# A graph network's first layer: the products that reorder a part of the edges issued in one piece, and a place's bits taken by one and-operation

## The chip, the cores and the metric

The kernel runs on one NeuronCore of one Trainium2 chip. The metric is the device time of one execution in microseconds (us), as the median of several executions. A profile of one execution stands beside it; its times are us from its first instruction, unless marked ns. PE is the engine of the matmuls (PEld its weight loads), DVE the vector engine, ACT the scalar engine, POOL the general one (here it issues the gathers of node rows), SP a queue that issues DMA transfers. Each engine works its instructions off in the program's order.

## The reference

A graph of N = 6250 nodes with 64 features and 206250 edges (src, dst), sorted by dst, with 64 attributes each. Three layers of an attention convolution:

```python
q = x @ Wq + bq; k = x @ Wk + bk; v = x @ Wv + bv
e = edge_attr @ We
alpha = sum(q[dst] * (k[src] + e), -1) / sqrt(64)
w = softmax of alpha over the edges of one dst
x = segment_sum((v[src] + e) * w, dst) + x @ Ws + bs
x = relu(x)                      # and a layer norm after layers 0 and 1
...
out = layernorm(x_in + log_softmax(x))
```

## The kernel before

**Tiling.** Edges go in tiles of 128, chunks of 6 tiles (768 edges, which touch at most 32 neighbouring nodes), and units of 4 chunks (LB = 4): 67 whole units and a small rest. In every layer a loop runs over the units. It holds four quarters (j = 0 to 3), one per chunk. In each, PE transposes the chunk's node features (`turn`, L1679, into bank ps_a), and over the quarters the scores of the unit before are made (`scores`, L1692, bank ps_s, in two halves), masked and reduced on DVE (`most`, L1706), exponentiated on ACT (L1720), transposed (`weights`, L1734, bank ps_p), copied to probT by ACT (L1737) and multiplied with the features (`sums`, L1746, bank ps_g). Node rows come in by gathers (POOL) or by **picks**: one-hot matmuls with node features that stay in SBUF (L1387, eight a pick, bank ps_s or ps_p by the quarter), whose result DVE copies out (L1356, L1359, `evacuate`).

**The reordering.** So that later layers can pick rows, layer 0 also puts each unit's edges into an order by their source node. That is the work of a `Move`, one per unit. It has four `Part`s: half h of a chunk's tiles and pair i of chunks (h, i = 0, 0; 0, 1; 1, 0; 1, 1). A part has three **steps** (HT = 3, t = 0 to 2), one tile of each of its two chunks at a time:
- `row` (L1074, DVE) makes two one-hots `hit` of 128 x 384: which place each edge of the tile goes to. They lie in 12 buffers and are made two steps ahead.
- `prepare` (L1042, L1045, DVE) splits the raw edge attributes of the part to come into three bf16 thirds, raw, rest and end.
- `products` (L1077 to L1102, PE) multiplies thirds and one-hots: six matmuls a step into one bank ps_x, two beside each other, one on columns 0 to 63 and one on columns 64 to 127. With the second pair (i = 1) come four more a step into ps_m, one per chunk, 32 columns each: `stamp` holds, for each edge, five bits of its place among the chunk's 32 nodes and numbers of its source. After the third step `drain` (ACT, L1115, L1118) copies ps_m to `to` and ps_x to `eT`, and sends eT to DRAM (L1121).
- `put` does, for the move before: `index` (L1165, L1167) with the first step, `shade` (L1152, from bank ps_m, copied by ACT at L1153) with the second and third step of part 0, and `across` (L1128, transposes of eT into ps_a, copied by ACT at L1136) with two steps each of part 0 and part 1.

**The mark.** For each 16 chunks (four units) `mark` works out the places, in 18 pieces, one a step (L887 to L1014). DVE and PE take turns in it. Its last pieces transpose the edges' places (L999) and break each into five bits: nine operations of 96 elements on DVE (L1008, L1010), written into `misc`, from which ACT fills the stamps (`impress`, L1064, L1065).

**What sets the order.** The order is written out by hand: the generator `sorter` makes one step at each `next`, and the loop of units calls it three times a quarter (`move`, L1817; six times in the first three units), twice ahead of the quarter's pick and once behind it. So one quarter works one part, and one unit one move. Each engine then follows that order and waits for the others only where data or a bank asks for it. Bank tags of PSUM: two buffers each for ps_a and ps_x, one each for ps_m, ps_s, ps_p and ps_g. ps_a serves nearly all transposes, the index and the mark.

Of the kernel before, what the change touches and what calls it, by code (L numbers as in the profile page):

```python
# [10 lines left out]
I32 = mybir.dt.int32  # L11
# [4 lines left out]
ALU = mybir.AluOpType  # L16
# [3 lines left out]
P = 128  # L20
D = 64
# [7 lines left out]
W = 32  # L29
BITS = 5  # L30
FAR = 2.0**100
GS = 4
LB = 4
TC = 6
CE = TC * P
HT = TC // 2
HE = HT * P
# [392 lines left out]
def main_path(  # L430
# [53 lines left out]
    nc = tc.nc  # L484
# [27 lines left out]
    const = ctx.enter_context(tc.tile_pool(name="const", bufs=1))  # L512
# [16 lines left out]
    def ps(tag):  # L529
        return psum.tile([P, 512], F32, tag=tag, name=f"ps_{tag}", bufs={"a": 2, "x": 2}.get(tag, 1))  # L530
# [5 lines left out]
    start = turns.tile([P, NK * CE], F32, name="start")  # L536
# [114 lines left out]
    for k in range(NK):  # L651
        n = min(P, NC - k * P)
# [80 lines left out]
    nc.vector.memset(code, 0.0)  # L733
    for j in range(LB):
        strip = slice(j * W, (j + 1) * W)
        for at in (j * (BITS + 1), P + j * W):
            nc.vector.tensor_copy(code[strip, at : at + BITS + 1], bit[strip, :])
# [108 lines left out]
    kbs = const.tile([P, NT, NP, LB], mybir.dt.uint8, name="kbs")  # L846
    four = const.tile([P, KB], F32, name="four")
    shift = const.tile([P, TC, 2], F32, name="shift")
    stamps = [const.tile([P, LB * TC, W], BF16, name=f"stamp{i}") for i in range(2)]

    def tools():
# [29 lines left out]
        for stamp in stamps:  # L881
            nc.vector.memset(stamp, 0.0)
            nc.vector.memset(stamp[:, :, ROW_ONE], 1.0)

    marks = {}

    def mark(g):  # L887
# [3 lines left out]
        n = m * TC  # L891
# [106 lines left out]
        for t in range(TC):  # L998
# [3 lines left out]
                ident[w0 : w0 + wide, w0 : w0 + wide],  # L1002
            )
        yield
        nc.vector.tensor_copy(v.rearrange("p (c t) -> p c t", t=TC), place)
        for b in reversed(range(BITS)):
            row = misc[:, b]
            nc.vector.tensor_scalar(row, v, 2.0**b, None, ALU.is_ge)  # L1008
            if b:
                nc.vector.scalar_tensor_tensor(v, row, -(2.0**b), v, ALU.mult, ALU.add)  # L1010
            if b == 2:
                yield
        marks[g] = misc, pos
        yield  # L1014

# [32 lines left out]
    class Move:  # L1048
# [25 lines left out]
                nc.vector.tensor_scalar(hit, ruler, self.pos[:, at : at + 1], None, ALU.is_equal)  # L1074
                self.hits[h, c, t] = hit

        def products(self, h, i, t):  # L1077

            if not t:
                self.px = ps("x")  # L1080
                if i:
                    self.pm = ps("m")
            for part in range(3):
                for j in range(2):
                    nc.tensor.matmul(  # L1085
                        self.px[j * D : (j + 1) * D, :HE],
                        self.parts[2 * h + i].thirds[part][:, j, t * D : (t + 1) * D],
                        self.hits[h, 2 * i + j, t],
                        start=(t == 0 and part == 0),
                        stop=(t == HT - 1 and part == 2),  # L1090
                    )
            if i:
                for c in range(LB):
                    nc.tensor.matmul(  # L1094
                        self.pm[c * W : (c + 1) * W, :HE],
                        self.stamp[:, c * TC + h * HT + t, :],
                        self.hits.pop((h, c, t)),
                        start=(t == 0),
                        stop=(t == HT - 1),
                    )  # L1100
            if t == HT - 1:
                self.drain(h, i)  # L1102

        def drain(self, h, i):

# [40 lines left out]
        def shade(self, h):  # L1146

            if not h:
                self.mask = tos.tile([P, CE], BF16, name="mask", bufs=1)
            pm = ps("m")  # L1150
            cols = slice(h * HE, (h + 1) * HE)
            nc.tensor.matmul(pm[:, :HE], codeW, self.to[:, cols], start=True, stop=True)  # L1152
# [51 lines left out]
    def sorter():  # L1204
# [16 lines left out]
        for stage in range(2):  # L1221
            todo[0].prepare(stage)
        moves[0].impress()
        for s in range(2):
            steps[s][0].move.row(steps[s][0].h, steps[s][0].i, steps[s][1])
        opened.append(True)
        yield
# [875 lines left out]
```

## Time and profile before

| | |
|---|---|
| median of 3 runs | 4206.91 us (4202.07 to 4214.05) |
| the profiled execution's own time | 4197.44 us |
| its span, first to last instruction | 4195.7 us |
| PE busy | 3513.2 us, 84% |
| DVE busy | 3452.3 us, 82% |
| ACT busy | 2347.5 us, 56% |
| POOL busy | 2563.3 us, 61% |
| mean granted PE clock | 0.953 |

Layer 0 ends near 1890 us; layers 1 and 2 take the rest. "Busy" counts the time in which an engine has an instruction under way. Idle time in a row's brackets is what the engine waited just before that instruction, with the operation that ended the wait. A row of several equal matmuls (x8) gives their time from the first start to the last end; successive rows of PE overlap, since one matmul drains while the next one runs, so lengths on PE are read from start to start. A float32 matmul counts as two, so a pick or a score product of 4 matmuls in the code is 8 in the trace.

### The profile page before, as it was taken

The page shows a single profiled execution, that of the slowest core. Times are in us where ns is not written, and L with a number is a line of the kernel's source. Part 1 is how long each engine was busy: PE and PEld are TensorE (multiplying, and loading weights), DVE is VectorE, ACT ScalarE, POOL GpSimd, SP SyncE. Part 2 cuts the span into 40 slices and gives each one's busy share as a digit, 9 for nine tenths or more (in the row PEclk, how much of TensorE's full clock was granted, in tenths as well). Part 3 has the DMA queues.
Part 4 walks back from the last instruction along what each step waited for, and adds up shares of the span by engine and source line. Part 5 has one row for each costly group of instructions (what it writes and reads, how often), then busy time and mean ns, then how long its engine had stood idle before and what let it go on. Part 6 is the DMA issues. An engine that isn't in the chain of part 4 may idle for free.

```text
span 4195.7 us, 109920 instructions
## 1 busy us (share of the span) xinstructions
PE 3513.2 (84%) x35239; PEld 2484.7 (59%) x35239; DVE 3452.3 (82%) x12154; ACT 2347.5 (56%) x5994; POOL 2563.3 (61%) x2510
## 2 busy tenths in 40 slices
PE   3878889998998998895988888888858888888886
PEld 2445555555555555553767667666647667666674
DVE  5678898889888898874888888888758888888886
ACT  0445555655565555563655555555535656666665
POOL 5466666666666666663766666666447666666662
PEclk9899999999999999996999999999979999999998
DMA  5666666667666667665777777777648777777774
GB/s 109 177 165 180 174 186 177 175 181 187 179 176 181 178 173 183 180 182 130 189 182 183 182 176 178 192 176 182 164 127 192 185 174 185 187 179 183 179 179 101
DMA packets 779286, 729.02 MB, mean 174 GB/s; under 512 B 483080, under 2 KB 607938, under 8 KB 778704
## 3 DMA queue, kind: packets, MB, share of 16 engines
q1 hardware_dynamic: 630436, 512.79, 49.9%
q0 software_dynamic: 80000, 82.08, 10.2%
q10 hardware_dynamic: 68268, 127.03, 8.4%
q8 instruction: 288, 4.72, 0.5%
q14 instruction: 294, 2.41, 0.2%
HBM read 562.78 MB, written 158.68 MB: 172 GB/s over the span
## 4 chain that ended last, share of the span: by engine, by line


## 5 line engine op out<-in xcount | busy, mean ns | idle before, releaser
L601 POOL DMA_INDIRECT feat<-x,gate x1328 | 1318.0, 992 | 729.0 <-ACT gate L633 356.4
L601 POOL DMA_INDIRECT feat<-in_x,gate x1100 | 1172.1, 1066 | 690.4 <-ACT gate L633 369.6
L1387 PE MATMUL ps_x<-parts,hot 128*128 128x256 f32 x7392 | 1084.9, 294 | 223.1 <-DVE feat L1359 185.9
L1387 PEld LDWEIGHTS ps_x<-parts,hot 128*128 128x128 f32 x7392 | 946.0, 193 | 383.0 <-issue 213.5
L1682 ACT COPY featT<-ps_a 64x384 f32<-64x384 f32 x1588 | 753.8, 475 | 372.9 <-PE ps_a L1679 351.5
L1359 DVE COPY_PREDICATED feat<-which,ps_x 128x128 f32<-128x128 int32 x2772 | 838.0, 302 | 95.5
L1335 DVE TENSOR_SCALAR hot<-keys,rank 128x512 fp32r<-128x512 f16 (+1 forms) x1304 | 507.3, 457 | 4.7 <-DMA keys<-keyS 4.7
L1074 DVE TENSOR_SCALAR hit<-ruler,pos 128x384 bf16<-128x384 f16 x1608 | 456.3, 325 | 6.3 <-PE ps_m L1094 5.4
L1679 PE MATMUL ps_a<-ident,feat 128*128 128x128 f32 x2380 | 420.9, 286 | 40.7 <-DMA feat<-x,src_b 31.9
L1679 PEld LDWEIGHTS ps_a<-ident,feat 128*128 128x128 f32 x2380 | 279.6, 145 | 226.0 <-issue 185.3
L1356 DVE COPY feat<-ps_x 128x128 f32<-128x128 f32 x924 | 263.9, 286 | 173.6 <-PE ps_x L1387 166.4
L1692 PE MATMUL ps_s<-featT,q 128*32 128x384 f32 x2134 | 289.5, 507 | 81.4 <-DMA featT<-eaS 43.1
L1720 ACT ACTIVATE prob<-prob,part 128x768 f32<-128x768 f32 x204 | 190.3, 933 | 232.0 <-DVE part L1719 200.5
L1746 PE MATMUL ps_g<-feat,probT 128*32 128x128 f32 x9672 | 311.7, 275 | 2.4 <-ACT probT L1737 2.4
L1085 PE MATMUL ps_x<-hit,raw 128*64 128x384 bf16 x1608 | 294.5, 362 | 0.5 <-DVE hit L1074 0.4
L1746 PEld LDWEIGHTS ps_g<-feat,probT 128*32 128x32 f32 x9672 | 261.9, 110 | 25.6 <-ACT probT L1737 4.1
L1085 PE MATMUL ps_x<-hit,rest 128*64 128x384 bf16 x1608 | 276.2, 340 | 0.0
L1085 PE MATMUL ps_x<-hit,end 128*64 128x384 bf16 x1608 | 275.6, 339 | 0.0
L1737 ACT COPY probT<-ps_p 128x384 f32<-128x384 f32 x399 | 191.8, 481 | 124.7 <-PE ps_p L1734 92.8
L1734 PE MATMUL ps_p<-ident,prob 128*128 128x128 f32 x1197 | 206.8, 283 | 9.7 <-ACT prob L1720 9.6
L1118 ACT COPY eT<-ps_x 128x384 f32<-128x384 f32 x268 | 129.3, 483 | 122.1 <-PE ps_x L1085 84.7
L1136 ACT COPY feat<-ps_a 128x384 f32<-128x384 f32 x256 | 122.1, 481 | 133.6 <-PE ps_a L1128 97.4
(266 smaller groups left out, 5167.9 us busy)
## 6 DMA issues: line engine op xcount, KB each, us to landing
featT<-eaS SPq DMA_DIRECT2D x792, 192.0 KB
feat<-eaP SPq DMA_DIRECT2D x134, 768.0 KB
keys<-keyS SPq DMA_DIRECT2D x132, 448.0 KB
raw<-in_ea SPq DMA_DIRECT2D x536, 96.0 KB
eaS<-eT ACTq DMA_DIRECT2D x134, 384.0 KB
eaP<-feat ACTq DMA_DIRECT2D x128, 384.0 KB
shade<-maskS SPq DMA_DIRECT2D x198, 192.0 KB
feat<-x,gate POOLq DMA_INDIRECT x1328
```

The lines of the kernel that those rows point to most:

```text
L601: nc.gpsimd.indirect_dma_start(out=feat[:, c, t, 0], out_offset=None, in_=xts[layer][:, :], in_offset=bass.IndirectOffsetOnAxis(ap=index[: ...
L1074: nc.vector.tensor_scalar(hit, ruler, self.pos[:, at : at + 1], None, ALU.is_equal)
L1085: nc.tensor.matmul(self.px[j * D : (j + 1) * D, :HE], self.parts[2 * h + i].thirds[part][:, j, t * D : (t + 1) * D], self.hits[h, 2 * i + ...
L1335: nc.vector.tensor_scalar(hot[:, h], keys[self.layer, k][:, first : first + n], rank[:, h : h + 1], None, ALU.is_equal)
L1356: nc.vector.tensor_copy(found, px[:, :, 0])
L1359: nc.vector.copy_predicated(found, which[:, first : first + 2, b].bitcast(I32).unsqueeze(2).to_broadcast([P, 2, D]), px[:, :, b],)
L1387: nc.tensor.matmul(px[:, v].rearrange("p b d -> p (b d)"), hot[:, h, (2 * pair + v) * P : (2 * pair + v + 1) * P], those[:, i, b0 + h * KB ...
L1679: nc.tensor.transpose(pt[:, t * P : (t + 1) * P], rows[:, 2 * t * D : 2 * (t + 1) * D], ident)
L1682: nc.scalar.copy(featT[:, :, h, :], pt[h * D : (h + 1) * D, : n * P].rearrange("d (i e) -> d i e", e=P))
L1692: nc.tensor.matmul(p_s[rows, :w], self.q[:, rows], self.featT[j][:, cols], start=True, stop=True)
L1734: nc.tensor.transpose(p_t[:, t, :n], self.prob[:n, at : at + P], ident[:n, :n])
L1746: nc.tensor.matmul(p_g[rows, :].rearrange("n (h d) -> n h d", h=2), self.probT[:, t, rows], batch[:, j, t], start=(t == 0), stop=(t == sel ...
```

## The change

Five edits, all in layer 0 or its setting up. `products` is called once a part, at its third step, and issues all of the part: 18 matmuls into ps_x, then 6 into ps_m, those of the part's own two chunks. The bank ps_m is now held from a move's part with i = 0 to the one with i = 1, and `shade` takes ps_a instead. One-hots are made three steps ahead (a part), and the next move's stamps are filled one step sooner. In the mark the five bits come from one and-operation with a table of the powers 1 to 16 and one ACT copy; each bit then stands as 0 or its power, and the table `codeW` that the mask is made with is scaled by the inverse powers (five one-column operations in the setting up, five more fill the powers).

```diff
         nc.vector.tensor_copy(v.rearrange("p (c t) -> p c t", t=TC), place)
-        for b in reversed(range(BITS)):
-            row = misc[:, b]
-            nc.vector.tensor_scalar(row, v, 2.0**b, None, ALU.is_ge)
-            if b:
-                nc.vector.scalar_tensor_tensor(v, row, -(2.0**b), v, ALU.mult, ALU.add)
-            if b == 2:
-                yield
+        bits = spare[:, 1 : BITS + 1].bitcast(I32)
+        nc.vector.tensor_tensor(
+            bits,
+            v.unsqueeze(1).to_broadcast([P, BITS, n]),
+            powers.unsqueeze(2).to_broadcast([P, BITS, n]),
+            ALU.bitwise_and,
+        )
+        nc.scalar.copy(misc[:, :BITS], bits)
+        yield
...
-        def products(self, h, i, t):
-
-            if not t:
-                self.px = ps("x")
-                if i:
-                    self.pm = ps("m")
-            for part in range(3):
-                for j in range(2):
-                    nc.tensor.matmul(
-                        self.px[j * D : (j + 1) * D, :HE],
...
-            if i:
-                for c in range(LB):
+        def products(self, h, i):
+
+            px = self.px = ps("x")
+            if not i:
+                self.pm = ps("m")
+            for t in range(HT):
+                for part in range(3):
+                    for j in range(2):
+                        nc.tensor.matmul(
+                            px[j * D : (j + 1) * D, :HE],
...
+            for t in range(HT):
+                for c in range(2 * i, 2 * i + 2):
                     nc.tensor.matmul(
                         self.pm[c * W : (c + 1) * W, :HE],
                         self.stamp[:, c * TC + h * HT + t, :],
...
-            if t == HT - 1:
-                self.drain(h, i)
+            self.drain(h, i)
...
-            pm = ps("m")
+            pm = ps("a")
...
-                if part is move.parts[3] and not t and n + 1 < len(moves):
+                if part is move.parts[2] and t == HT - 1 and n + 1 < len(moves):
...
-                if s + 2 < len(steps):
-                    ahead_of, u = steps[s + 2]
+                if s + HT < len(steps):
+                    ahead_of, u = steps[s + HT]
...
-                move.products(part.h, part.i, t)
+                if t == HT - 1:
+                    move.products(part.h, part.i)
```

Line numbers below 733 stay. Later lines stand four to ten further on in the changed kernel (`products` 1077 becomes 1087, `turn` 1679 becomes 1689).

**PE, first quarter of a unit, from the chunk's transposes to the next scores.** Before (of rows that repeat, one stands for all; ps_x are the products, L1152 the shade, L1128 the across, L1387 the pick):

```order
L1679 MATMUL ps_a<-ident,feat 128x128 x3
L1165 MATMUL ps_a<-to,keyc 4x4x64
L1167 MATMUL ps_g<-pickc,to 128x12
L1085 MATMUL ps_x<-hit,raw 64x384
L1152 MATMUL ps_m<-to,codeW 128x384
L1128 MATMUL ps_a<-ident,eT 128x128 x3
L1387 MATMUL ps_p<-parts,hot_11341 128x256 x8
L1692 MATMUL ps_s<-featT,q 32x384 x4
```

And with the change:

```order
L1689 MATMUL ps_a<-ident,feat 128x128 x3
L1174 MATMUL ps_a<-to,keyc 4x4x64
L1176 MATMUL ps_g<-pickc,to 128x12
L1161 MATMUL ps_a<-to,codeW 128x384
L1137 MATMUL ps_a<-ident,eT 128x128 x3
L1397 MATMUL ps_p<-parts,hot_11307 128x256 x8
L1095 MATMUL ps_x<-hit,raw 64x384
L1104 MATMUL ps_m<-hit,stamp_265 32x384
L1702 MATMUL ps_s<-featT,q 32x384 x4
```

Before, six products (L1085) stand after the index, six more before the pick, and six after the second pair of shade and across. Now index, shade and across follow each other directly, then the pick, then shade and across once more, and only then all 18 products and the six of the stamps. Every product before the pick in this order now takes ps_a, or ps_g.

**PE, last quarter, from the prob transposes (L1734, with the change L1744) on.** Before:

```order
L1734 MATMUL ps_p<-ident,prob 128x128 x3
L1679 MATMUL ps_a<-ident,feat 128x128 x3
L1085 MATMUL ps_x<-hit,raw 64x384
L1094 MATMUL ps_m<-hit,stamp_259 32x384
L1387 MATMUL ps_p<-parts,hot_24820 128x256 x8
```

And with the change:

```order
L1744 MATMUL ps_p<-ident,prob 128x128 x3
L1689 MATMUL ps_a<-ident,feat 128x128 x3
L1397 MATMUL ps_p<-parts,hot_24737 128x256 x8
L1095 MATMUL ps_x<-hit,raw 64x384
L1104 MATMUL ps_m<-hit,stamp_265 32x384
```

The products of two steps stood between the transposes into ps_p and the pick that uses ps_p again; now only the chunk's three transposes do.

**DVE, the end of the mark.** Before:

```order
L1005 COPY spare<-ps_a 128x96
L1008 TENSOR_SCALAR misc<-spare 128x96
L1010 SCALAR_TENSOR_TENSOR spare<-misc,spare 128x96
L1074 TENSOR_SCALAR hit<-ruler,pos 128x384 x2
L1356 COPY feat<-ps_s 128x2x64
```

And with the change:

```order
L1013 CAST spare<-ps_a 128x96
L1015 TENSOR_TENSOR spare<-spare,powers 128x480
L1084 TENSOR_SCALAR hit<-ruler,pos 128x384 x2
L1366 COPY feat<-ps_s 128x2x64
L1369 COPY_PREDICATED feat<-which,ps_s 128x2x64 x3
```

Nine narrow operations (L1008 five times, L1010 four times, in two groups with the one-hots between) become one of 480 elements. Apart from that DVE's order stays as it was; its one-hots are those of a step further on.

More of the change, by code (lines that the diff above doesn't have):

```diff
@@ L735, in main_path @@
         strip = slice(j * W, (j + 1) * W)
-        for at in (j * (BITS + 1), P + j * W):
-            nc.vector.tensor_copy(code[strip, at : at + BITS + 1], bit[strip, :])
+        nc.vector.tensor_copy(code[strip, j * (BITS + 1) : (j + 1) * (BITS + 1)], bit[strip, :])
+    for b in range(BITS):
+        nc.vector.tensor_scalar(bit[:, b : b + 1], bit[:, b : b + 1], 2.0**-b, None, ALU.mult)
+    for j in range(LB):
+        strip = slice(j * W, (j + 1) * W)
+        nc.vector.tensor_copy(code[strip, P + j * W : P + j * W + BITS + 1], bit[strip, :])
     pc = ps("a")
@@ L883, in tools @@
             nc.vector.memset(stamp[:, :, ROW_ONE], 1.0)
+        for b in range(BITS):
+            nc.vector.memset(powers[:, b : b + 1], 1 << b)
     marks = {}
@@ L1075, in row @@
                 self.hits[h, c, t] = hit
-        def products(self, h, i, t):
-            if not t:
-                self.px = ps("x")
-                if i:
-                    self.pm = ps("m")
-            for part in range(3):
-                for j in range(2):
-                    nc.tensor.matmul(
-                        self.px[j * D : (j + 1) * D, :HE],
[L1087 to L1091, printed above, removed]
-            if i:
-                for c in range(LB):
+        def products(self, h, i):
[7 more added lines that the diff above has]
+                            px[j * D : (j + 1) * D, :HE],
+                            self.parts[2 * h + i].thirds[part][:, j, t * D : (t + 1) * D],
+                            self.hits[h, 2 * i + j, t],
+                            start=(t == 0 and part == 0),
+                            stop=(t == HT - 1 and part == 2),
+                        )
+            for t in range(HT):
+                for c in range(2 * i, 2 * i + 2):
                     nc.tensor.matmul(
@@ L1223, in sorter @@
         moves[0].impress()
-        for s in range(2):
+        for s in range(HT):
             steps[s][0].move.row(steps[s][0].h, steps[s][0].i, steps[s][1])
```

2 lines of the change are left out of this document (added).

## The prediction

> **What bounds the kernel now.** The page's chain of waits is empty, so I read the table of stretches, cut at the start of each unit's sums (L1746), then the waits, then the order of time inside one unit. The change touches layer 0 alone, its loop of units. Four neighbouring units (us from the start, length, then busy time of PE, PEld, DVE, ACT, POOL, the granted clock, DMA):
>
> ```profile
> 1280.29:1302.84 22.55, 21.45 (x237) 13.04 (x233) 17.97 (x63) 14.52 (x38) 15.49 (x16) 1.00 0.88 223
> 1302.84:1333.07 30.23, 25.31 (x259) 14.68 (x251) 28.33 (x96) 15.64 (x41) 23.59 (x20) 1.00 0.64 170
> 1333.07:1362.92 29.85, 24.51 (x244) 14.93 (x245) 25.82 (x92) 15.32 (x42) 13.64 (x15) 0.94 0.55 146
> 1362.92:1385.20 22.28, 21.67 (x240) 13.54 (x236) 19.89 (x70) 14.98 (x39) 16.70 (x17) 1.00 0.81 206
> ```
>
> The pattern repeats: a mark serves 16 chunks, four units, and its 18 steps cover one and a half units of 12. So two units in four are **plain**: PE is busy 21.5 of 22.4 us and sets the length, DVE has over 2 us to spare. In the **first mark unit** DVE (28.3 of 30.2) sets it and PE has 5 us to spare. In the second it goes from DVE to ACT to PE. The waits from 400 to 1700 us (engine, line waited for, us, times, longest) say the same:
>
> ```profile
> PE ps_a L923 <- DVE kinds L916: 23.5, 12, 2.9
> PE ps_s L1692 <- DVE most L1706: 20.6, 25, 1.7
> PE ps_a L1128 <- ACT featT L1682: 14.2, 17, 2.2
> PE ps_a L1165 <- ACT featT L1682: 11.4, 18, 1.0
> DVE feat L1356 <- PE ps_s L1387: 36.1, 54, 1.5
> DVE feat L1356 <- PE ps_p L1387: 19.7, 37, 1.4
> ```
>
> The first two are PE ahead of DVE, in mark units; the next two are PE waiting for ACT to empty one of the two ps_a banks; the last two are DVE waiting for picks, mostly in plain units, where it costs nothing. No row has PE waiting for a one-hot. So what counts is whether PE's work in plain units gets shorter and whether its waits for ACT grow.
>
> **PE's own work.** Five rows of one step (start, length), and two where two steps stand together already:
>
> ```profile
> 1300.03 0.36 PE L1085 MATMUL ps_x<-hit,raw 128*64 128x384 bf16 x2
> 1300.22 0.33 PE L1085 MATMUL ps_x<-hit,rest 128*64 128x384 bf16 x2
> 1300.38 0.33 PE L1085 MATMUL ps_x<-hit,end 128*64 128x384 bf16 x2
> 1300.64 0.35 PE L1094 MATMUL ps_m<-hit,stamp 128*32 128x384 bf16 x4
> 1300.92 1.21 PE L1387 MATMUL ps_p<-parts,hot 128*128 128x256 f32 x8
> ...
> 1355.91 0.33 PE L1085 MATMUL ps_x<-hit,end 128*64 128x384 bf16 x2
> 1356.08 0.33 PE L1085 MATMUL ps_x<-hit,raw 128*64 128x384 bf16 x2
> ```
>
> A pair on the two halves of the columns takes 0.16 us from start to start, and each change to another shape about 0.1 more (0.26, 0.28). A step of i = 0 costs 0.61, one of i = 1 0.89: six of each, 9.0 us a unit. A part in one piece: 0.19 + 7 x 0.163 + 0.26 = 1.59 for nine pairs, so ten shape changes a unit are saved. But the stamps' products stand two beside each other instead of four. Their 24 a unit take 12 rounds instead of 6: three rounds a part, 2 x 0.165 + 0.28 = 0.61. Four parts: 8.8 us, **0.2 us less a unit**. No row shows two strips of 32 returned to at once. If they ran as fast as four abreast it were 0.33 less a part, if one by one at 0.26 then 0.95 more; I take 0.165 because the pairs above return to the same columns after 0.16.
>
> **ps_a in a unit's first quarter.** What the moved steps issue here: index, two shades, two acrosses, with two steps' products between them as filler. PE, then ACT:
>
> ```profile
> 1282.35 0.55 PE L1679 MATMUL ps_a<-ident,feat 128*128 128x128 f32 x3
> ...
> 1283.14 0.31 PE L1167 MATMUL ps_g<-pickc,to 128*128 128x12 bf16 x6
> 1283.37 0.35 PE L1085 MATMUL ps_x<-hit,raw 128*64 128x384 bf16 x2
> ...
> 1283.99 0.34 PE L1152 MATMUL ps_m<-to,codeW 128*128 128x384 bf16 x1
> 1284.16 0.49 PE L1128 MATMUL ps_a<-ident,eT 128*128 128x128 f32 x3
> ...
> 1285.19 1.20 PE L1387 MATMUL ps_p<-parts,hot 128*128 128x256 f32 x8
> 1286.23 0.34 PE L1152 MATMUL ps_m<-to,codeW 128*128 128x384 bf16 x1
> ```
> ```profile
> 1282.93 0.96 ACT L1682 COPY featT<-ps_a 64x384 f32<-64x384 f32 x2 [0.81 <-PE ps_a L1679]
> ...
> 1284.01 0.57 ACT L1186 CAST key<-ps_a 4x512 f16<-4x512 f32 x1
> ...
> 1285.88 0.48 ACT L1136 COPY feat<-ps_a 128x384 f32<-128x384 f32 x1
> ```
>
> Now the shade asks for a ps_a bank, and the filler is gone. PE has the index done at 1283.37; the shade needs the bank of the unit's transposes, free when ACT's featT copies end at 1283.89: 0.52 us of waiting. The shade (0.17) ends at 1284.06; the across needs the keys' bank, copied by 1284.58: 0.52 more. Across (1.03 to the picks, less a step's 0.61) and picks (1.04) run to 1286.04, the second shade to 1286.21, the second across waits for the feat copy's end at 1286.36: 0.15. Together **1.2 us a plain unit**. The products come afterwards with nothing left to hide under. That this bank wait is real the L1165 row above shows: where another transpose stands between, the keys' product waits for these very copies, 18 times, 0.6 us each.
>
> **The last quarter.** The picks there use bank p, just after the prob transposes:
>
> ```profile
> 1298.34 0.55 PE L1734 MATMUL ps_p<-ident,prob 128*128 128x128 f32 x3
> 1298.72 0.49 PE L1679 MATMUL ps_a<-ident,feat 128*128 128x128 f32 x3
> ...
> 1299.14 0.35 PE L1085 MATMUL ps_x<-hit,raw 128*64 128x384 bf16 x2
> ```
> ```profile
> 1298.88 0.48 ACT L1118 COPY eT<-ps_x 128x384 f32<-128x384 f32 x1
> 1299.39 0.33 ACTq L1121 DMA_DIRECT2D eaS<-eT  x1
> 1299.76 0.48 ACT L1737 COPY probT<-ps_p 128x384 f32<-128x384 f32 x1 [0.40 <-issue]
> ```
>
> Two steps' products covered the copy to probT. Now the picks are ready 0.80 us after 1298.34 and must wait for it. ACT still has to do eT (which may start some 0.4 before, when the last pair is done), the issue of eaS and probT: -0.4 + 0.48 + 0.33 + 0.48, about 0.9 to 1.1. I take **0.3 us**; the ends are 0 and 1.1 (with ACT as late as in these rows, done at 1300.24 against 1299.14).
>
> **The mark's bits** (groups from 400 to 1700 us):
>
> ```profile
> L1008 DVE TENSOR_SCALAR misc<-spare 128x96 bf16<-128x96 f32 x65 | 14.4, 221 | 1.8
> L1010 DVE SCALAR_TENSOR_TENSOR spare<-misc,spare 128x96 f32<-128x96 bf16 x52 | 13.7, 264 | 1.8
> L946 DVE TENSOR_TENSOR spare<-ps_a,kinds 128x480 f16<-128x480 f32 x36 | 23.3, 647 | 1.0 <-PE ps_a L944 0.9
> ACT misc L985 <- DVE spare L984: 24.7, 12, 3.4
> ```
>
> Nine operations go, 5 x 221 + 4 x 264 = 2.16 us a mark; one of 480 elements comes. It isn't in the trace; between 0.22 (the narrow row) and 1.1 (five narrow ones) I take L946's 0.65, the same width. DVE saves 1.5 us a mark, 17 marks (268 chunks by 16), 26 us. It falls in the second quarter of the second mark unit, where PE comes out of a wait late and DVE behind it:
>
> ```profile
> 1349.58 0.55 PE L1128 MATMUL ps_a<-ident,eT 128*128 128x128 f32 x3 [2.21 <-ACT featT L1682]
> ...
> 1351.11 2.08 PE L1387 MATMUL ps_s<-parts,hot 128*128 128x256 f32 x8
> 1353.22 0.29 DVE L1356 COPY feat<-ps_s 128x128 f32<-128x128 f32 x1 [1.08 <-PE ps_s L1387]
> ```
>
> DVE waits 1.08 us for the picks just behind the bits, so I count the saving as nothing; without that cover it is the 26 us. The new ACT copy (estimate 0.6 us, by the 384-wide 0.48) must wait for the and-operation with feat, eT and featT copies queued behind it, as misc does at L985 (2 us each time, PE then waits for ps_a). ACT reaches it after the feat copy of the 1349.58 across, DVE sooner: nothing, at worst 15 x 2 = 30 us. In this quarter the step whose products stood in the shadow of the 2.21 us now follows: 0.4 us.
>
> **At nothing.** The one-hots lie in 12 buffers, two parts: each now waits until PE has done nearly the whole part before the last. Behind it on DVE stand rest, end and the copies out of the picks' banks, for which later picks wait. DVE's spare time in plain units covers it; in first mark units PE is ahead. Uncovered it is up to 1 us a quarter there, 60 us. On SP's queue the loads of raw wait for the same part's last reading, four parts before their use, and nothing is late there. Setting up (ten one-column operations, two one-hots sooner): 1 to 3 us.
>
> **Sum.** After the first three units, 61 units: 30 plain, 15 and 15 marked. Plain: -0.2 + 1.2 + 0.3 = 1.3. The L1128 and L1165 waits, 25.6 us over some 49 units, are 0.5 each, and half may fall together with the new ones: 1.05, times 30 = 32 us. First mark unit: 0, since PE's later arrival shortens the waits for L916 and L1706. Second: 0.4 in its second quarter, the last quarter's 0.3, -0.2: 0.5 x 15 = 7. With 1 for setting up, **+40 us**: on the profiled run's 4197.4 that is 4237; on the median of the runs shown, 9.5 above it, 4247.
>
> **Rivals.** (1) **DVE sets more than I think, and it becomes faster.** If the mark units are DVE's to the end, the 26 us come through, and 61 x 0.2 = 12 us of PE's work with them, provided ACT empties ps_a in time: 4207 - 26 - 12 = 4169. Picks ahead of products also shorten the 55.8 us of DVE's waits at L1356. Against it: those waits lie where PE is full, and the ps_a wait has rows. It decides from where the new waits stay under 0.5 us a plain unit. Chance 0.15. (2) **Both cancel**: 30 x 1.05 against 26: within 13 us of 4207. Chance 0.11. (3) **The clock falls more often.** After the 2.21 us wait eight picks took 2.08 us, not 1.21; with its neighbours some 1.4 us. Once more in each of 15 mark units: +21, 4268. PE's idle time is gathered into fewer, longer pieces, which speaks for it; in plain units the new pieces are short and the clock is 1.00. Chance 0.10. By the Trainium skill (TensorE: Matmul & The Clock Gate, Part 1) an idle window of about 3.4 us halves the clock until a busy one has passed; the 2.08 agrees. (4) **Stamps' weights aren't loaded under the products before**: 0.26 a round, not 0.165, 0.2 a part, 0.8 a unit; plain units alone 24 us, 4271. The pairs at 0.16 speak against it. Chance 0.05. The Trainium skill (same page, Part 3, The mechanism) has loads overlap only where the row groups differ, which would be this case; the pairs share their rows and don't wait.
>
> The forecast's own chance is 0.59, its own range 4225 to 4270. Less than 0.3% (13 us) this measurement can't tell from no change. Faster 0.15, same 0.11, slower 0.74. The range, 4185 to 4290, leaves out the best of (1), and the upper ends of the last quarter and the one-hots together.
>
> **What would show it.** Plain units of 23 to 24 us, not 22.4; in them PE waits of about 0.5 us at the shade and the across for ACT's featT and key copies, and at the last picks for probT. The mark's and-operation near 0.65 us, second mark units no shorter, first ones near 30 us. Three stamp rounds in 0.5 to 0.6 us. Plain units at 22 us, or mark units 1.5 us shorter, would prove me wrong; so would DVE waiting long at the one-hots in the first mark unit.

## The result, and the profile after

| | before | after |
|---|---|---|
| median of 4 runs, us | 4210.48 (4202.07 to 4223.55) | 4275.22 (4271.27 to 4280.43) |
| ratio, 95% interval | | 1.0159 (1.0134 to 1.0184) |
| the profiled execution's own time, us | 4197.44 | 4272.08 |
| busy PE / DVE / ACT, us | 3513.2 / 3452.3 / 2347.5 | 3531.2 / 3425.5 / 2357.6 |
| mean granted PE clock | 0.953 | 0.942 |

The change costs 65 us; 40 were forecast. DVE lost 27 us of work, as worked out for the mark's bits, and that bought no time (e1 below). The two profiled executions lie 74 us apart: 57 us up to layer 1's first sums (2001.45 us before, 2058.87 after), and 17 behind them, where nothing was edited. That last stretch took 2194 us before and 2211 after, and 2178 to 2196 in the profiles of e1 to e10, so the 17 us are taken for the scatter of single executions and not for the change.

The table of stretches of the kernel after, cut at the start of each unit's sums (now L1756), has the columns of the prediction's: length, then busy time of PE, PEld, DVE, ACT and POOL, granted clock, DMA share and GB/s. First the four neighbours that answer to the prediction's four, then a plain unit in which a group of nodes is finished beside the usual work:

```profile
1323.08:1345.36 22.28, 20.81 (x236) 14.08 (x237) 17.93 (x63) 14.38 (x38) 16.04 (x16) 1.00 0.88 237
1345.36:1377.88 32.52, 27.30 (x263) 16.80 (x261) 28.34 (x95) 14.96 (x40) 21.72 (x19) 0.95 0.56 147
1377.88:1405.45 27.57, 23.34 (x239) 15.66 (x237) 24.64 (x85) 16.54 (x45) 16.05 (x15) 0.94 0.60 159
1405.45:1428.18 22.73, 21.30 (x240) 14.55 (x240) 19.57 (x70) 14.95 (x39) 16.71 (x16) 1.00 0.80 208
...
662.01:695.11 33.10, 27.15 (x252) 18.74 (x252) 21.56 (x80) 17.54 (x41) 19.27 (x20) 0.80 0.56 150
```

The same finishing unit before:

```profile
647.59:674.54 26.95, 24.96 (x252) 15.69 (x248) 20.40 (x77) 17.40 (x41) 16.68 (x17) 0.94 0.66 175
```

The plain units hardly moved (22.55 and 22.28 before, 22.28 and 22.73 now). The first mark unit is 2.3 us longer, and the finishing unit 6.2 us, at a clock of 0.80. So the bulk isn't where the prediction looked. All 50 units from the 7th on, by kind (numbers counted from 0; means of such lengths, us; "finishing" are the four plain units with products `ve, wT`, L1547):

| | number | before | after | all together |
|---|---|---|---|---|
| plain | 22 | 22.82 | 23.40 | +12.7 |
| finishing | 4 | 25.47 | 30.70 | +20.9 |
| first mark unit | 12 | 30.89 | 32.08 | +14.3 |
| second mark unit | 12 | 28.43 | 28.60 | +2.0 |
| the 50 units | | 1315.8 | 1365.7 | +49.9 |

The first seven units add 11 us (223.9, now 235.0).

PE's waits from 400 to 1700 us (bank, line, what was waited for: us, times, longest) after the change:

```profile
PE ps_p L1397 <- ACT probT L1747: 27.0, 44, 3.2
PE ps_a L1137 <- ACT featT L1692: 22.2, 25, 1.6
PE ps_a L1137 <- ACT key L1195: 17.0, 26, 1.7
PE ps_a L949 <- ACT featT L1692: 15.3, 12, 1.4
...
PE ps_s L1702 <- DVE most L1716: 6.5, 11, 0.7
...
PE ps_a L930 <- DVE kinds L923: 5.4, 5, 2.3
```

The two waits for DVE that led before, 23.5 us for `kinds` and 20.6 for `most`, are down to 5.4 and 6.5. In their place PE waits for ACT to empty a bank, in three places: at the last picks (L1397), at the across (L1137) and at the mark's L949.

### The profile page after: what moved, and what is told of

Its sections match the earlier page's. It is cut to its first block, busy times and chain, and to the rows that moved or that the text cites. A ratio compares the mean times of both kernels' runs of the same rounds, so it can differ in the third digit from the quotient of the medians.

```text
span 4270.0 us, 109764 instructions
## 1 busy us (share of the span) xinstructions
PE 3531.2 (83%) x35239; PEld 2576.5 (60%) x35239; DVE 3425.5 (80%) x12028; ACT 2357.6 (55%) x6011; POOL 2580.1 (60%) x2510
## 4 chain that ended last, share of the span: by engine, by line
## 5 line engine op out<-in xcount | busy, mean ns | idle before, releaser
L601 POOL DMA_INDIRECT feat<-in_x,gate x1100 | 1185.9, 1078 | 734.0 <-ACT gate L633 423.1
L1397 PE MATMUL ps_x<-parts,hot 128*128 128x256 f32 x7392 | 1090.1, 295 | 222.2 <-DVE feat L1369 186.0
L1397 PEld LDWEIGHTS ps_x<-parts,hot 128*128 128x128 f32 x7392 | 952.0, 194 | 382.8 <-issue 214.2
L1084 DVE TENSOR_SCALAR hit<-ruler,pos 128x384 bf16<-128x384 f16 x1608 | 450.7, 321 | 36.0 <-PE ps_m L1104 35.8
L1702 PE MATMUL ps_s<-featT,q 128*32 128x384 f32 x2134 | 321.4, 498 | 67.6 <-DMA featT<-eaS 50.0
L1756 PE MATMUL ps_g<-feat,probT 128*32 128x128 f32 x9672 | 335.2, 276 | 3.6 <-ACT probT L1747 3.6
L1756 PEld LDWEIGHTS ps_g<-feat,probT 128*32 128x32 f32 x9672 | 275.7, 110 | 28.6 <-ACT probT L1747 5.8
L1137 PE MATMUL ps_a<-ident,eT 128*128 128x128 f32 x804 | 156.9, 310 | 86.0 <-ACT featT L1692 25.4
L1124 ACT CAST to<-ps_m 128x384 bf16<-128x384 f32 x134 | 64.2, 479 | 268.6 <-PE ps_m L1104 260.5
L1744 PE MATMUL ps_p<-ident,prob 128*128 128x128 f32 x1197 | 206.1, 282 | 7.7 <-ACT prob L1730 7.6
```

Source lines behind the costliest of these rows:

```text
L601: nc.gpsimd.indirect_dma_start(out=feat[:, c, t, 0], out_offset=None, in_=xts[layer][:, :], in_offset=bass.IndirectOffsetOnAxis(ap=index[: ...
L1397: nc.tensor.matmul(px[:, v].rearrange("p b d -> p (b d)"), hot[:, h, (2 * pair + v) * P : (2 * pair + v + 1) * P], those[:, i, b0 + h * KB ...
L1702: nc.tensor.matmul(p_s[rows, :w], self.q[:, rows], self.featT[j][:, cols], start=True, stop=True)
L1744: nc.tensor.transpose(p_t[:, t, :n], self.prob[:n, at : at + P], ident[:n, :n])
L1756: nc.tensor.matmul(p_g[rows, :].rearrange("n (h d) -> n h d", h=2), self.probT[:, t, rows], batch[:, j, t], start=(t == 0), stop=(t == sel ...
```

## Where the time went in the trace after

A plain unit, PE by time (start, length, line, in brackets the wait):

```profile
1327.21 0.32 PE L1161 MATMUL ps_a<-to,codeW 128*128 128x384 bf16 x1 [0.50 <-ACT featT L1692]
1327.91 0.55 PE L1137 MATMUL ps_a<-ident,eT 128*128 128x128 f32 x3 [0.38 <-ACT key L1195]
...
1336.61 0.67 PE L1104 MATMUL ps_m<-hit,stamp 128*32 128x384 bf16 x6
1337.20 0.55 PE L1744 MATMUL ps_p<-ident,prob 128*128 128x128 f32 x3
...
1342.60 1.22 PE L1397 MATMUL ps_p<-parts,hot 128*128 128x256 f32 x8 [0.58 <-ACT probT L1747]
```

The three waits stand where they were forecast, 0.50, 0.38 and 0.58 us; the one at the second across is missing. Three stamp rounds take 0.59 us, from 1336.61 to 1337.20 (0.61 forecast).

ACT ahead of those last picks, and a row of the kernel before:

```profile
1340.51 0.41 ACT L1074 COPY stamp<-misc 128x120 bf16<-128x120 bf16 x1
1340.83 0.34 ACT L1075 COPY stamp<-misc 128x72 bf16<-128x72 bf16 x1
1341.19 0.48 ACT L1127 COPY eT<-ps_x 128x384 f32<-128x384 f32 x1
...
1342.07 0.48 ACT L1747 COPY probT<-ps_p 128x384 f32<-128x384 f32 x1 [0.40 <-PE ps_a L1689]
```
```profile
1301.22 0.43 ACT L1064 COPY stamp<-misc 128x120 bf16<-128x120 bf16 x1
```

The two copies that fill the next move's stamps come one step sooner with the change. Before, they stood behind probT (1301.22, probT at 1299.76); now they take ACT 0.68 us, from 1340.51 to 1341.19, ahead of eT and so of probT. The prediction's chain for this wait (eT, the issue of eaS, probT) doesn't hold them. Its transposes (L1744) end at 1341.69, so without the copies probT could have started about then and not at 1342.07: an estimate of 0.38 us of the 0.58. No run moved the copies back; e3 and e8 keep them here, under cover of products.

The finishing unit, PE first, then ACT:

```profile
670.87 0.90 PE L1137 MATMUL ps_a<-ident,eT 128*128 128x128 f32 x3 [1.54 <-ACT key L1195]
671.43 2.06 PE L1397 MATMUL ps_p<-parts,hot 128*128 128x256 f32 x8
...
690.07 2.07 PE L1397 MATMUL ps_p<-parts,hot 128*128 128x256 f32 x8 [3.24 <-ACT probT L1747]
692.07 0.53 PE L1095 MATMUL ps_x<-hit,raw 128*64 128x384 bf16 x2
692.39 0.53 PE L1095 MATMUL ps_x<-hit,rest 128*64 128x384 bf16 x2
```
```profile
669.92 0.30 ACT L1478 ACTIVATE dev<-mv,eps 128x4 f32<-128x4 f32 x1 [2.44 <-DVE mv L1476]
...
686.73 0.48 ACT L1127 COPY eT<-ps_x 128x384 f32<-128x384 f32 x1
689.17 0.33 ACTq L1130 DMA_DIRECT2D eaS<-eT  x1
689.54 0.48 ACT L1747 COPY probT<-ps_p 128x384 f32<-128x384 f32 x1 [2.33 <-DMA eaP<-feat]
```

Two waits are long here. The first is at the across of the first quarter: ACT waits 2.44 us for DVE's `mv` of the finished group's layer norm (L1476), and the keys' copy stands behind that (670.24 to 670.81). The across waits 1.54, 1.70, 1.71 and 1.71 us for the keys in the four finishing units; before the change it never waited there. (The clock is half from 668.17 to 675.00, so it had fallen ahead of this wait, and the first picks take 2.06 us.)

The second is at the last picks. ACT is done with eT at 687.21, and its issue of eaS starts 1.96 us later, with probT behind it. The kernel before has the same stall in this unit, and on PE it shows as

```profile
672.63 1.21 PE L1387 MATMUL ps_p<-parts,hot 128*128 128x256 f32 x8 [0.83 <-ACT probT L1737]
```

because two steps' products stood in front of those picks. Bare, with no such products in front, the wait is 3.24 us, and behind it picks take 2.07 us and pairs stand 0.32 us apart: half the clock, until the unit's end. In the four finishing units this wait was 0.83, 0.41 and 0.25 us and in one nothing; now it is 3.24, 1.86, 1.88 and 1.76. Only in the first of them is the issue 2 us late; in the other three it follows eT by 0.5 to 0.6 us.

The first mark unit, PE by time:

```profile
1359.60 0.55 PE L1137 MATMUL ps_a<-ident,eT 128*128 128x128 f32 x3 [1.05 <-ACT featT L1692]
...
1366.16 0.36 PE L949 MATMUL ps_a<-left,ones 1*128 1x480 bf16 x1 [1.38 <-ACT featT L1692]
...
1367.30 1.74 PE L1397 MATMUL ps_s<-parts,hot 128*128 128x256 f32 x8
1368.97 0.53 PE L1095 MATMUL ps_x<-hit,raw 128*64 128x384 bf16 x2
1369.29 0.53 PE L1095 MATMUL ps_x<-hit,rest 128*64 128x384 bf16 x2
```

The bare places go on in the second and third quarter: the across waits 1.05 us for the featT copies in each of the 12, and the mark's L949 1.38 us (0.76 in two of them). PE's time to spare goes into such waits, and then the clock halves.

## The experiments

Each kernel ran beside the kernel before on its own chip, so ratios are compared. Medians of the kernel before were 4177 to 4179 us there, 0.5% under the 4197 us of the profile in the first row, so lengths of units are compared with that row only beyond half a per cent (0.15 us of a mark unit, 6 us of the 50). Lines are a few off between kernels. All runs but e11 and e12 are in one table; kinds as above, "half clock" is 2 x (1 - granted clock) x length summed over the 50 units, since the clock in the traces is either whole or half. Lengths and half clock are of one profile each: e8 and e10, alike from the 13th move on, differ by 9 and 34 us in the last two columns.

| | ratio (95%) | plain | finishing | first mark | second mark | 50 units | half clock |
|---|---|---|---|---|---|---|---|
| before | 1 | 22.82 | 25.47 | 30.89 | 28.43 | 1315.8 | 85 |
| after | 1.0159 (1.0134 to 1.0184) | 23.40 | 30.70 | 32.08 | 28.60 | 1365.7 | 144 |
| e1 bits alone | 1.0026 (1.0006 to 1.0046) | 22.54 | 25.78 | 30.60 | 28.99 | 1314.1 | 103 |
| e2 products alone | 1.0167 (1.0135 to 1.0200) | 23.46 | 30.51 | 31.84 | 29.39 | 1372.9 | 147 |
| e3 products first | 0.9999 (0.9978 to 1.0020) | 22.40 | 24.23 | 31.64 | 26.59 | 1288.5 | 74 |
| e4 last picks in bank s | 1.0085 (1.0055 to 1.0114) | 22.27 | 26.45 | 31.68 | 29.41 | 1328.8 | 123 |
| e5 shade in bank m | 1.0133 (1.0104 to 1.0161) | 22.97 | 28.23 | 32.24 | 28.25 | 1344.1 | 111 |
| e6 both | 1.0037 (1.0021 to 1.0054) | 22.09 | 24.56 | 31.97 | 28.79 | 1313.2 | 88 |
| e7 filler | 1.0153 (1.0128 to 1.0178) | 23.53 | 30.28 | 31.69 | 29.22 | 1369.6 | 147 |
| e8 behind the index | 0.9965 (0.9948 to 0.9982) | 22.01 | 24.98 | 31.13 | 26.22 | 1272.3 | 65 |
| e9 e8 without bits | 0.9952 (0.9933 to 0.9971) | 22.27 | 25.43 | 31.02 | 26.25 | 1279.0 | 61 |
| e10 e8, early moves as before | 0.9973 (0.9958 to 0.9988) | 21.99 | 25.53 | 31.36 | 26.61 | 1281.5 | 99 |

**e1, the bits alone**: the kernel before with the change's edits of the mark and of codeW, and no other.

> The kernel before with the mark's bits made by the and-operation, products untouched. Theory A (the moved products alone cost the time: PE stands in front of ACT's copies in a unit's first and last quarter, and its clock falls behind the longer waits): the bits' 26 us of DVE time are hidden behind PE and ACT, 0 to -8 us, some 4203 to 4211. Theory C (ACT's new copy, which stands in front of the copies out of ps_a, costs part of it): +10 to +30 us, above 4220. Theory D (DVE sets the second mark units): -15 to -26 us, below 4195.

No gain; if anything a loss of 11 us (2 to 19), in the range that Theory C gave. But its mechanism isn't there: ACT waits 0.1 us in all for the and-operation. Where the 11 us lie stays open; the steady stretch shows none of them.

**e2, the products alone**: the change without those edits.

> The change without its edit of the mark's bits: nine DVE operations a mark as before, products in one piece. Theory A: the loss stays whole, 4270 to 4290, ratio 1.014 to 1.019. Theory C: ACT's copy is part of the loss, so it is smaller here, 4245 to 4265. Theory D: DVE's 26 us come back on top, 4290 to 4305.

The loss is whole, as Theory A has it. The bits have no part in it; what is left is the products' new form and place, with the bank of the shade, the one-hots and the stamps.

**e3, the products first.**

```diff
+                if not t:
+                    move.products(part.h, part.i)
                 if n:
                     moves[n - 1].put(part.h, part.i, t)
                 if t == HT - 1:
-                    move.products(part.h, part.i)
+                    move.drain(part.h, part.i)
```

> The whole change, but a part's products are issued at its first step, ahead of the put and the pick, and drained at its last step as before. Stamps are two abreast and one-hots are three steps ahead as in the change. Theory A (place): PE has 2.1 us of work under ACT's copies again, the waits of 0.5 us at the shade and the across and of 0.57 us at the last quarter's picks go; 4195 to 4215, ratio 0.997 to 1.001. Theory B (form: two stamps abreast, one-hots tied up for a part, no products between two transposes): the place doesn't matter, 4250 to 4280. In between: PE now stands in front of DVE's one-hots in the first mark units, which would show as waits for L1084.

The loss is gone though the form stayed: one piece, two stamps abreast, one-hots a part ahead, stamps filled a step sooner, shade in ps_a. The place decides, and Theory B falls. The expected waits for L1084 didn't come; in mark units PE waits for DVE's mark instead, longer than before the change (23.5 and 20.6):

```profile
PE ps_a L930 <- DVE kinds L923: 34.0, 12, 3.2
PE ps_s L1703 <- DVE most L1717: 30.4, 43, 2.3
```

**e4, the last picks in another bank.**

```diff
-                    bank = "x" if self.layer else "pssp"[self.quarter]
+                    bank = "x" if self.layer else "psss"[self.quarter]
```

> The change with the last quarter's picks in bank s (free since the scores were read) and not in bank p, which the copy to probT empties. Theory A: the wait for probT (0.57 us in each of some 60 units, 2 to 3 us in the seven units that finish a group of nodes, and the halved clock behind these) goes: 30 to 45 us less than the change, 4230 to 4245. Theory B: PE loses nothing there that it would not lose elsewhere, 4265 to 4280.

31 us less than the change (0.74% of 4210), the lower edge of Theory A. The finishing units lose 4.3 us each and the plain ones 1.1. In the second mark units a wait came in another place, 1.6 us in each:

```profile
PE ps_s L1702 <- issue: 19.5, 12, 1.6
```

The view names no releaser ("issue"). By the rows it is bank s: in one of these units DVE's copies of the last picks out of it end at 498.89, and the next scores, which take it, start at 498.99.

**e5, shade in bank m.**

```diff
-            pm = ps("a")
+            pm = ps("m")
```

> The change with the shade back in bank m (which the products of a unit's first part now take only behind both shades); all else as changed. Theory A (the first quarter's loss is the order: nothing stands between index, shade and across): the shade no longer waits for the featT copies, but the across behind it does, 0.35 us instead of 0.52 + 0.52; with the mask copies gone from ps_a some 0.5 to 0.8 us a unit less, ratio 1.006 to 1.011 against 1.016 of the change. Rival A2 (the across takes over the whole wait): 1.014 to 1.017. Rival A3 (the bank is all of the first quarter's loss): below 1.004.

A gain of 0.26%, nearer to A2 than to A, since the intervals of e5 and the change overlap. The trace shows what took the place of the shade's wait for featT (e5's waits):

```profile
PE ps_a L1137 <- ACT featT L1692: 24.8, 37, 1.1
PE ps_m L1161 <- ACT mask L1162: 16.7, 20, 2.1
PE ps_m L1104 <- ACT mask L1162: 15.4, 8, 4.2
```

The across waits for featT 37 times instead of 25, and the second shade and the first stamps wait for the mask copies.

**e6, both banks.**

> Both: shade in bank m and the last quarter's picks in bank s. The last quarter alone took the ratio from 1.016 to 1.0085. Theory A: the two gains add up, 0.999 to 1.003. If the two waits lie behind one another (what the one frees the other holds), 1.004 to 1.008.

The gains add up and a little more (0.74 and 0.26% from 1.59% leave 0.59%; measured 0.37, 0.21 to 0.54). The measured ratio lies between the two ranges that were expected, and its interval reaches into both. Plain and finishing units are better than before the change; the first mark units still stand at 31.97, since their waits at the across and at L949 were not touched.

**e7, a filler ahead of L949** (results that nobody reads):

```diff
+        filler = ps("x")[:, : CELLS * H].rearrange("p (q h) -> p q h", q=CELLS)
+        for _ in range(6):
+            nc.tensor.matmul(filler, ones, kinds[:, :, 0], start=True, stop=True)
         for i in range(HT):
             before = ps("a")[:, : CELLS * H].rearrange("p (q h) -> p q h", q=CELLS)
```

> The change with six products of 128x480 that nobody reads (1.2 us) on PE ahead of the mark's L949, where PE stands still for 1.4 us in each first mark unit. Theory K (PE's clock falls behind this wait and the halved clock is what makes the first mark units 1.2 us longer): the picks behind L949 take 1.2 us and not 1.7 to 2.1, the products behind stand 0.16 us apart and not 0.32, the 15 units get 1 to 2 us shorter, ratio 1.009 to 1.013. Rival W (the wait itself is the loss, the clock isn't): nothing gained, 1.015 to 1.019.

The rows of the same first mark unit:

```profile
1364.13 0.36 PE L952 MATMUL ps_a<-left,ones 1*128 1x480 bf16 x1 [0.16 <-ACT featT L1695]
...
1365.27 1.28 PE L1400 MATMUL ps_s<-parts,hot 128*128 128x256 f32 x8
1366.48 0.36 PE L1098 MATMUL ps_x<-hit,raw 128*64 128x384 bf16 x2
1366.67 0.33 PE L1098 MATMUL ps_x<-hit,rest 128*64 128x384 bf16 x2
```

The picks are whole again, 1.28 us, and the next pair follows at 0.19. Picks over 1.3 us in the 12 first mark units fell from 8 to 2 of 48, and the half-clock time in them from 38 to 21 us. Yet these units got at most 0.4 us shorter (0.15 against e2's), and the ratio didn't move: here the clock is a small part, and W was right. For the other units the run says nothing: over the 50 units the half-clock time stayed (147 us), since it rose in the second mark units from 68 to 82.

**e8, the products behind the index.**

```diff
                 if n:
                     moves[n - 1].put(part.h, part.i, t)
+                if not t:
+                    move.products(part.h, part.i)
                 if t == HT - 1:
-                    move.products(part.h, part.i)
+                    move.drain(part.h, part.i)
```

> The whole change, a part's products at its first step but behind the index (in e3 they stood ahead of it, so the first mark units waited for DVE, whose mark needs the index), drained at the last step. Theory A: all of e3's cover stays and the mark begins as early as before: the first mark units come from 31.6 back to 30.6 to 30.9 us, 12 to 20 us less than e3; ratio 0.993 to 0.998. Rival: the featT copies hold the index as before, and what is won in the second mark units is lost at the scores, 0.999 to 1.002.

Faster than both kernels, 0.9965, 1.9% better than the change by place alone. The mark, which needs the index, starts earlier than in e3 (PE's wait for `kinds` 22.8 us against 34.0): first mark units 31.1 us against e3's 31.6, where 30.6 to 30.9 were expected. That is 6 of the 16 us between the two in the 50 units; the rest is spread over the other kinds. PE's waits of e8 in the same stretch:

```profile
PE ps_s L1703 <- DVE most L1717: 23.8, 30, 2.3
PE ps_a L930 <- DVE kinds L923: 22.8, 12, 3.1
PE ps_a L1173 <- ACT featT L1693: 13.3, 18, 2.0
```

They are those of the kernel before; those for probT, at L949 and at the across have left the top. The second mark units are 2.2 us shorter than before the change.

**e9, e8 without the bits.**

> The products behind the index at a part's first step (as in e8, ratio 0.9965), but without the edit of the mark's bits. Theory A with hidden bits (their 26 us of DVE lie under PE and ACT in every version; alone they gave 1.0026): the same as e8 to within 0.2%, 0.994 to 0.998. Rival D2 (with PE's waits gone the second mark units are DVE's, so the bits are worth their time there): 8 to 20 us more than e8, 0.998 to 1.001, and the second mark units 0.7 to 1.5 us longer than e8's 26.2 us.

No loss without them, second mark units 26.25 against 26.22: DVE doesn't set them here either.

**e10, e8 with the first 12 moves' products issued step by step.**

```diff
-                if not t:
-                    move.products(part.h, part.i)
+                if n < 12:
+                    move.products(part.h, part.i, [t])
+                elif not t:
+                    move.products(part.h, part.i, range(HT))
```

> As e8, but the first 12 moves issue their products step by step (behind the put, stamps still two abreast), as before. Theory S (in the first units, where loads and one-hots come late, a part in one piece waits for its last one-hot; e8 stood 9 to 12 us behind the kernel before when the steady stretch began): the first seven units come back to about 224 to 227 us from 233, 5 to 10 us less than e8, ratio 0.994 to 0.996. Rival: the early loss is the other edits' (one-hots three steps ahead, shade in ps_a), nothing gained: 0.996 to 0.998.

The first seven units came back as Theory S says (223.6 us; e8 233.0, before 223.9), so the piece waits there. The time didn't follow: the 50 units behind took 9 us more than e8's in these single profiles, and the intervals overlap.

**e11 and e12, both kernels again**, as a base for the unit lengths.

> The kernel before, unchanged, profiled where e1 to e10 were, since its first profile is from other runs (4205 to 4211 us there, 4177 to 4179 here). If the 30 us between lie in all layers alike, its units 7 to 56 take 1303 to 1312 us, not 1315.8, and layer 0's last sums start at 1905 to 1920; if they lie elsewhere, 1316 and 1925 again. Slow picks (over 1.3 us) in those units: 6 to 12 of some 200.

> The changed kernel, unchanged, in the same place: units 7 to 56 take 1350 to 1366 us, 45 to 55 more than e11; units that finish a group of nodes 2.5 to 4 us longer, first mark units 1 to 1.5, plain ones 0.4 to 1.0, second mark units 0 to 0.5; slow picks 20 to 32 of some 200.

Both failed as a base: they took 5.47 and 5.50 ms there at a granted clock of 0.86, and the kernel before took 5.46 ms beside them. So how far e8's 43 us in the 50 units carry over to its 15 us in all (7 to 22) isn't settled.

## Why the prediction was right or wrong

**Direction and mechanism: right; the size in part luck.** e2 and e3 show that the moved products cost the time, by their place. The waits stand at the shade, the across and the last picks, behind the copies that were named. But of the 33 us that the sum has for these 50 units (23 plain, 4 finishing, 0 first mark, 6 second mark) some 19 came where they were put, and 35 of the 49.9 came from the two kinds that the sum held at 4 and at nothing. One error stands against the other, and still the measured 4275 us lies above the forecast's own range of 4225 to 4270.

**Plain units: over-estimated.** The first quarter was put at 1.2 us and is 0.88 (0.50 + 0.38; the second across doesn't wait), the last quarter at 0.3 and is 0.58. Most of that 0.58, an estimated 0.38, is the stamps' copies, which the chain left out; the rest is near the forecast. Waits grew by 0.83 us a plain unit (0.93 to 1.76 by all brackets), and the length by 0.58, not 1.05. For 26 plain and finishing units that is 27 us forecast; the 22 plain ones gave 12.7.

**Finishing units: the term that was missing.** The sum treated them as plain, 4 x 1.05 = 4 us; they cost 20.9. PE's waits in them went from 1.41 to 4.88 us a unit by all brackets, 1.8 us more at the last picks and 1.7 us more at the first quarter's across. The prediction bounded the last quarter by 1.1 us from a plain unit's ACT rows. In finishing units ACT comes later to probT (behind an issue of eaS that is 0.5 to 2 us late), which before hid under the two steps' products, so the wait is up to 3.2 us. The across was put at 0.52 us everywhere, but in these units the keys' copy stands behind ACT's wait for the layer norm. The half clock comes on top (half-clock time in the four: 7 us, now 34); no run separates it from the waits here. e4, which takes the wait for probT away in all units, gives back 31 us of 65, more than the other edit of a bank; by unit lengths some 17 us in the 4 finishing and 25 in the 22 plain units, less 10 lost in the second mark units.

**First mark units: the step that failed.** "First mark unit: 0, since PE's later arrival shortens the waits for L916 and L1706." It did shorten them (44.1 to 11.9 us from 400 to 1700 us), but the new waits are more than that reserve: all brackets in such a unit went from 4.32 to 5.04 us. Only the first quarter's were counted, not the 1.05 us at the second quarter's across and the 1.38 at L949, where the same filler had stood. 0 forecast, 14.3 measured. e7 puts the clock's share at no more than 0.4 of the 1.2 us; that the rest is these waits is argued from e8, in which they are gone and the units are back at 31.1, with as much half-clock time in them as after the change (41 us against 38).

**Second mark units**: 6 forecast for these 12, 2.0 measured. **Early units**: 1 us for setting up forecast, 11 measured. The one piece makes them, not its place: in e8 they stay at another place (233.0 us), and in e10, where the first 12 moves issue their products step by step, they vanish (223.6).

**Bits: right.** The and-operation takes 0.67 us (0.65 estimated) and ACT's copy 0.59 (0.6):

```profile
L1015 DVE TENSOR_TENSOR spare<-spare,powers 128x480 int32<-128x480 int32 x12 | 8.1, 674 | 1.3
L1021 ACT CAST misc<-spare 128x480 bf16<-128x480 int32 x12 | 7.1, 594 | 6.6 <-DVE spare L1015 6.6
```

Their 26 us bought nothing in e1, in the change (against e2) or in e8 (against e9).

**The rivals.** (1) and (2) fell with the result. (3), the clock, is real as a follower: half-clock time went from 85 to 144 us, and at half speed 59 us hold up to 30 us of PE's work. It goes away with the waits (88 in e6, 65 in e8). Only the first mark units had a test of the clock by itself (e7), and there it decided little; in the finishing and second mark units, which hold 48 of the 59 us, its share stays open. The prediction's "the 2.08 agrees" holds for the halving alone: before the fall at 1350.63 PE wasn't idle for 3.4 us, it was busy for 1.20 of the 3.41 us ahead of it. (4), stamps' weights exposed, fell: two pairs after the first of three rounds add 0.17 us each (0.67 - 0.33, halved), not 0.26. That agrees with the other branch of the rule that was set against it: the Trainium skill (TensorE: Matmul & The Clock Gate, Part 3, The mechanism) also lets a load run ahead into the background weight buffer. One-hots cost little: DVE waited 14.2 us for L1104 from 400 to 1700 us, and e3 and e8 keep them a part ahead at no loss.

## What to carry to other kernels

Work that stands between a bank's writer and its next user is cover: before gathering it, list every place it leaves, in every kind of unit, and price each bare place by the latest that its releaser comes in any unit, not in a typical one, with the copies that the change itself moves ahead of that releaser. A reserve on an engine covers the sum of all new waits in that unit, so add them up before calling them free. If gathered, the piece belongs ahead of the first bare place and behind what another engine is waiting for.

## What the runs showed of the hardware

The half clock came after waits far shorter than it lasts: in the first mark unit the longest wait is 1.38 us and ends at 1366.16, and the clock is half from 1367.90 to 1371.32:

```profile
1364.49:1367.90 3.41, 2.04 (x12) 1.05 (x11) 3.30 (x14) 2.95 (x11) 2.50 (x4) 1.00 0.82 188
1367.91:1371.31 3.40, 3.40 (x22) 2.18 (x22) 3.30 (x10) 0.29 (x2) 2.79 (x3) 0.50 0.49 113
```

In the 12 traces of the table every stretch of one clock lasts a whole multiple of 3.41 us. In the 3.41 us ahead of a fall PE had been busy for part of the time, here for 2.04 us; in the median of the 18 falls from 400 to 1700 us before the change it was 49%, of the 26 after it 51% (over 70% ahead of two of these). So what went ahead of a fall was as a rule a stretch that PE filled about half, not one long wait.

Small products of other columns run between each other, as the rows of a plain unit show, where six stamps and eight scores (four in the code; a pick is eight in the code as in the trace) together took 1.25 us from 1331.41 to 1332.66. Apart they take more: the stamps 0.59 (1336.61 to 1337.20), the scores 0.79 (1357.21 to 1358.00, in the first mark unit):

```profile
1331.41 0.50 PE L1104 MATMUL ps_m<-hit,stamp 128*32 128x384 bf16 x4
1331.60 0.52 PE L1702 MATMUL ps_s<-featT,q 128*32 128x384 f32 x2
1331.75 0.33 PE L1104 MATMUL ps_m<-hit,stamp 128*32 128x384 bf16 x2
1331.91 0.81 PE L1702 MATMUL ps_s<-featT,q 128*32 128x384 f32 x6
1332.66 0.55 PE L1689 MATMUL ps_a<-ident,feat 128*128 128x128 f32 x3
```

What ACT's issue of eaS waits for, 2 us in the first finishing unit before and after the change alike, stays open: behind it the trace names another transfer each time (eaP<-feat after the change, keys<-keyS before it), and it wasn't tried.
